# A graph-attention layer: block sums in chains, nodes ordered by one-hot products, first rows gathered ahead of the loop

## The chip, the cores and the metric

The kernel runs on one core of a Trainium2 chip. The metric is device time in microseconds (us) for one execution. Before the change it took 1119.08 us, the median of three runs (1115.03 to 1124.09). "Fast" is the state of a run in which nothing disturbed it; comparisons use fast runs.

## The reference, cut to what matters

Four graph layers work on 2708 nodes with 128 features and a dense 2708 x 2708 matrix, all in float32. The change lies in layer 1, an attention layer:

```python
XW    = X @ W
s_col = XW @ a[0, :f];  s_row = XW @ a[0, f:]
den   = exp(leaky_relu(s_row[:, None] + s_col[None, :], 0.01))
num   = A @ den
att   = where(num != 0, den / where(num != 0, num, 1.0), 0.0)
H     = A @ (att @ XW)
```

`den` has a simple form: where `s_row + s_col` is positive it is a product of two exponentials, elsewhere a product of two others. So if the nodes are sorted by `s_col`, then for a block of neighbouring columns each row uses one form for the whole block, except for the few rows whose change-over falls into the block. The kernels use this.

## The kernel before

Nodes are sorted and cut into blocks (`NB`, of `BJ` columns; 43 blocks of 64 before). For each block the sum over the rows that do not change inside it is taken by one dense product over the whole matrix (two weight columns per block: "the pass"). It goes to `carry`, two rows per block. The pass goes through the matrix in six chunks of up to 512 columns; a panel is four tiles of 128 rows of one chunk, loaded together. The rows that change inside a block, at most `KC` = 126 of them, are gathered from memory one by one. Together they are 128 rows, which one product per block (`num`) weighs. Two blocks make one step, and the columns are done in two halves `h`.

The rows stand in a pool of three buffers, which layer 0, the pass and the loop share in turn:

```python
stream = ctx.enter_context(tc.tile_pool(name="stream", bufs=3))
```

The loop stands in one side of a branch. The other side serves data in which some block has more than 126 such rows; it is not taken here.

```python
over = nc.values_load(flag[0:1, 0:1], min_val=0, max_val=N)
with tc.If(over > KC) as full:
    ...                                  # the dense way, not taken here
with full.Else():
    ...
    for h in range(2):
        hacc = ops.tile([P, 3 * CW], F32, tag="hacc", name="hacc")
        for q in range(NQ):
            rows = stream.tile([P, 2, HALF], F32, tag="strip", name="rows")
            for n, b in enumerate(pair):
                nc.gpsimd.indirect_dma_start(          # 126 rows of the matrix
                    out=rows[:KC, n, :], in_=adj_half[:, :],
                    in_offset=bass.IndirectOffsetOnAxis(ap=slot_i[h][:KC, b : b + 1], axis=0), ...)
                nc.sync.dma_start(rows[KC : KC + 2, n, :], carry[2 * b : 2 * b + 2, ...])
            for c0, w, bufs in ((0, WIDE, 2), (WIDE, NARROW, 1)):
                num = ops.tile([P, w], F32, tag=f"num{w}", name="num", bufs=bufs)
                ...                      # num[block] = lw[block].T @ rows
                mix(w, q, num, ...)      # 1/num, weights, hacc += xws.T @ err
```

## Time and profile before

| part of the profiled run before | from, us | length, us |
|---|---|---|
| layer 0 and the ordering by ranks | 0 | 438 |
| start and pass for block sums | 438.1 | 110.6 |
| loop, first `num` product to the copy after the last `hacc` | 548.7 | 232.5 |
| layers 2 and 3 with the rest of layer 1 | 781.2 | 338.2 |

These are two groups of the page (line, engine, operation, count, busy time in us and mean in ns, then the engine's idle time just before them and what ended most of it), and then TensorE's rows of one loop step (start, duration):

```profile
L1035 POOL DMA_INDIRECT rows<-in_adjT,slot_i x86 | 120.7, 1404 | 107.9 <-PE num L1048 79.9
L1048 PE MATMUL num<-rows,lw 128*64 128x512 f32 (+2 forms) x516 | 117.0, 558 | 6.7 <-DMA rows<-carry 3.7
```

```profile
638.13 2.50 PE L1048 MATMUL num<-rows,lw 128*64 128x330 f32 x12
640.56 2.54 PE L977 MATMUL hacc<-err,xws 128*128 128x512 f32 x6
```

GpSimd waits for TensorE to release a buffer, 79.9 us in all. The products are idle 6.7 us in total, 3.7 of them for the carried rows.

### The profile page before, as it was taken

How to read it: one execution, taken by the hardware profiler on the slowest of the kernel's cores; microseconds unless marked ns; L12 is line 12 of the kernel's file. 1: busy time of each engine (PE TensorE's matmuls, PEld its weight loads, DVE VectorE, ACT ScalarE, POOL GpSimd, SP SyncE). 2: the span in 40 equal slices, each digit the busy share in tenths (PEclk: the TensorE clock that was granted, in tenths of full speed). 3: DMA queues.
4: the chain of work that ended last, by engine and by line, in shares of the span. 5: the costliest groups of instructions: out<-in, count | busy, mean ns of one | idle time of the engine just before them, and what ended most of it. 6: DMA issues, size and time to landing. Idle time of an engine off the chain costs nothing.

```text
span 1119.4 us, 10743 instructions
## 1 busy us (share of the span) xinstructions
PE 1044.2 (93%) x3495; PEld 494.5 (44%) x3495; DVE 642.7 (57%) x1381; ACT 306.1 (27%) x569; POOL 299.4 (27%) x296
## 2 busy tenths in 40 slices
PE   0899999999999975999799999998999999999997
PEld 0346544444345654333333333333444644465445
DVE  6885549999636679403099999997311212122132
ACT  0000145555202434000165656664110100011000
POOL 4000000000477772772355655660010100000000
PEclk9999999999999995999999999998999999998999
DMA  9996320000576660797545534454475766563754
GB/s 349 354 316 222 125 101 1 1 0 1 178 274 201 184 207 13 230 304 236 164 121 148 176 96 129 164 171 142 150 236 186 227 227 219 173 227 117 263 166 129
DMA packets 110245, 193.89 MB, mean 173 GB/s; under 512 B 14156, under 2 KB 47106, under 8 KB 109926
## 3 DMA queue, kind: packets, MB, share of 16 engines
q1 hardware_dynamic: 91046, 151.12, 40.7%
q0 software_dynamic: 19136, 42.01, 12.0%
q8 instruction: 29, 0.48, 0.2%
q14 instruction: 34, 0.28, 0.1%
HBM read 217.20 MB, written 4.30 MB: 198 GB/s over the span
## 4 chain that ended last, share of the span: by engine, by line
PE 51%; issue 4%; DMA 4%; DVE 2%; POOL 1%; ACT 1%; POOLq 0%; DVEq 0%; ACTq 0%
PE acc L186 32%; PE hacc L977 8%; PE num L1048 8%; DMA rows<-in_adjT,slot_i 2%; DMA part<-in_adjT 1%; PE mis L259 1%; POOL rows L1035 1%; DVE mask L692 1%; PE mis L1110 0%; PE mis L1063 0%; DMA got<-y_rows,where 0%; ACT junk L710 0%; ACT hT L220 0%; PE mis L1076 0%; DVE mask L697 0%
## 5 line engine op out<-in xcount | busy, mean ns | idle before, releaser
L186 PE MATMUL acc<-part,y 128*128 128x512 f32 (+2 forms) x384 | 156.0, 550 | 2.1 <-DMA part<-in_adjT 1.6
L1035 POOL DMA_INDIRECT rows<-in_adjT,slot_i x86 | 120.7, 1404 | 107.9 <-PE num L1048 79.9
L1048 PE MATMUL num<-rows,lw 128*64 128x512 f32 (+2 forms) x516 | 117.0, 558 | 6.7 <-DMA rows<-carry 3.7
L977 PE MATMUL hacc<-err,xws 128*128 128x512 f32 (+3 forms) x264 | 113.6, 567 | 2.2 <-DVE err L972 1.8
L574 PE MATMUL acc<-zT,z 128*128 128x512 f32 (+4 forms) x264 | 106.9, 552 | 0.0
L602 POOL DMA_INDIRECT got<-y_rows,where x88 | 93.0, 1057 | 29.6 <-issue 11.9
L186 PEld LDWEIGHTS acc<-part,y 128*128 128x128 f32 x384 | 70.4, 191 | 64.5 <-issue 53.9
L970 DVE TENSOR_TENSOR err<-inv,num 128x1024 f32<-128x1024 f32 (+1 forms) x88 | 74.5, 856 | 27.1 <-DMA rows<-in_adjT,slot_i 21.0
L966 ACT ACTIVATE inv<-num 128x1024 f32<-128x1024 f32 (+1 forms) x88 | 64.3, 734 | 88.4 <-PE num L1048 86.6
L575 ACT COPY key<-acc 128x512 f32<-128x512 f32 (+3 forms) x132 | 70.2, 534 | 58.1 <-issue 29.8
L392 PE MATMUL acc<-part,y 128*128 128x512 f32 (+2 forms) x192 | 82.4, 582 | 2.2 <-DVE y L233 2.2
L977 PEld LDWEIGHTS hacc<-err,xws 128*128 128x128 f32 (+1 forms) x264 | 47.1, 192 | 80.4 <-issue 41.8
L186 PE MATMUL acc<-part,lc 128*86 128x512 f32 (+2 forms) x192 | 76.2, 553 | 3.3 <-DVE lc L876 2.5
L186 PE MATMUL acc<-part,xs 128*128 128x512 f32 (+2 forms) x192 | 78.6, 552 | 0.1
L972 DVE SCALAR_TENSOR_TENSOR err<-gb,g_inv,err 128x1024 f32<-128x1024 f32 (+1 forms) x88 | 77.1, 918 | 0.0
L536 POOL TENSOR_TENSOR y<-xs,d2inv 128x2176 f32<-128x2176 f32 (+1 forms) x2 | 4.6, 2322 | 264.3 <-ACT d2inv L534 264.3
L186 PE MATMUL acc<-part,mixed 128*128 128x512 f32 (+2 forms) x192 | 75.0, 545 | 0.2 <-DMA part<-in_adjT 0.2
L971 DVE SCALAR_TENSOR_TENSOR err<-err,inv 128x1024 f32<-128x1024 f32 (+1 forms) x88 | 71.8, 857 | 0.0
L574 PEld LDWEIGHTS acc<-zT,z 128*128 128x128 f32 (+1 forms) x264 | 47.0, 186 | 53.8 <-issue 48.4
L220 ACT COPY hT<-acc 128x512 f32<-128x512 f32 (+2 forms) x18 | 9.6, 534 | 220.1 <-PE acc L186 203.2
L967 ACT ACTIVATE inv<-inv 128x1024 f32<-128x1024 f32 (+1 forms) x88 | 67.3, 768 | 2.6
L576 DVE MAX8 near<-key 128x8 f32<-128x2708 f32 (+1 forms) x22 | 65.3, 2970 | 3.4 <-ACT key L575 3.4
(239 smaller groups left out, 1215.5 us busy)
## 6 DMA issues: line engine op xcount, KB each, us to landing
part<-in_adjT SPq DMA_DIRECT2D x102, 1024.0 KB
part<-in_adjT SPq DMA_DIRECT2D x24, 768.0 KB
part<-in_adjT SPq DMA_DIRECT2D x24, 552.0 KB
res<-in_adjT SPq DMA_DIRECT2D x4, 1280.0 KB
got<-y_rows,where POOLq DMA_INDIRECT x88, 3.9
rows<-in_adjT,slot_i POOLq DMA_INDIRECT x86, 5.8
rows<-carry SPq DMA_DIRECT2D x86, 10.6 KB
xws<-by_rank POOLq DMA_DIRECT2D x1, 1365.0 KB, 10.1
```

The costliest lines, as they stand in the source:

```text
L186: nc.tensor.matmul(accs[c][: lhsT.shape[-1], :w], lhsT=lhsT, rhs=src, start=start, stop=stop)
L392: nc.tensor.matmul(accs[c][:, : cw[c]], lhsT=y[:, i, :], rhs=src[:, : cw[c]], start=first, stop=last)
L574: nc.tensor.matmul(pks[c][:p, : cw[c]], lhsT=z2[:, :p], rhs=zT[:, cs], start=False, stop=True)
L575: nc.scalar.copy(key[:p, cs], pks[c][:p, : cw[c]])
L602: nc.gpsimd.indirect_dma_start(out=got[:p, :], out_offset=None, in_=y2_rows[:, :], in_offset=bass.IndirectOffsetOnAxis(ap=where[:p, t, k : ...
L967: nc.scalar.activation(inv[:p], inv[:p], AF.Exp, scale=-1.0)
L970: nc.vector.tensor_mul(err[:p], inv[:p], num[:p, :w])
L971: nc.vector.scalar_tensor_tensor(err[:p], err[:p], 2.0, inv[:p], op0=ALU.subtract, op1=ALU.mult)
L972: nc.vector.scalar_tensor_tensor(err[:p], gb[:p, col : col + w], g_inv[:p, q : q + 1], err[:p], op0=ALU.max, op1=ALU.mult)
L977: nc.tensor.matmul(haccs[:, o:e], lhsT=xws[:p, q, :D], rhs=err[:p, o:e], start=(q == 0), stop=(q == NQ - 1))
L1035: nc.gpsimd.indirect_dma_start(out=rows[:KC, n, :], out_offset=None, in_=adj_half[:, :], in_offset=bass.IndirectOffsetOnAxis(ap=slot_i[h][ ...
L1048: nc.tensor.matmul(num[n * BJ : n * BJ + bw[b], o:e], lhsT=lw[:, b, : bw[b]], rhs=rows[:, n, c0 + o : c0 + e], start=True, stop=True,)
```

## The change

The change has four aims. The pass becomes shorter: only the head of each chain of four blocks gets its sum from the dense product (22 columns of weights, padded to 32, in place of 86), and in the loop each block's product also yields the sum of the next block of its chain. Nodes are put in order by one-hot products on TensorE in place of 44 scatters by GpSimd through memory. The loop's order is written out by hand. And the rows of the first two steps are gathered ahead of the branch. The core of the diff, with cuts marked:

```diff
-BJ = 64
+BJ = 62
+CH = 4
 ...
-        by_panels(lambda i: lc[:, i, :, :].rearrange("p b s -> p (b s)"), end_carry)
+            nc.tensor.matmul(                                    # block sums, 4 column groups
+                sums_of[c][32 * g : 32 * g + 32, : cw[c]], lhsT=lc[rows, i, :], rhs=src, ...)
 ...                                                              # then one product folds the 4 groups
+        def into_places(out, at, values):                        # one-hot products for scatters
+                nc.vector.tensor_tensor(hot[:, :n, :], iota..., at[:, t0:t1, None]..., op=ALU.is_equal)
+                    nc.tensor.matmul(out[:, :width], lhsT=hot[...], rhs=values[...], ...)
-        scatter(by_slot, pos_u, val)
 ...
+    def load(i):
+        h, q = steps[i]
+        rows[i] = stream.tile([P, 2, HALF], F32, tag="strip", name="rows")
+        for n in range(2):
+            nc.gpsimd.indirect_dma_start(out=rows[i][:KC, n, :], ...)
+            nc.sync.dma_start(rows[i][KC : KC + 2, n, :], carry[2 * b : 2 * b + 2, ...])
+        if h == 0:
+            gather_xw(q)                                         # one more gather a step
+    load(0)
+    load(1)
     mT = wide.tile([P, N], F32, tag="wide", name="mT")
     over = nc.values_load(flag[0:1, 0:1], min_val=0, max_val=N)
     with tc.If(over > KC) as full:
 ...
     with full.Else():
-            for h in range(2): ... for q in range(NQ): rows = stream.tile(...)
+            with tc.manual_schedule(engines={e.engine for e in engines}):
+                find_num(0, "wide")
+                for i, (h, q) in enumerate(steps):
+                    if i + 2 < len(steps):
+                        load(i + 2)
+                    find_num(i, "narrow")
+                    find_num(i + 1, "wide")
+                    add(i - 1)
+                    ...
+                        keep(i, piece, errs[piece])              # a sum to the next block of the chain
```

## The prediction

> **What bounds the kernel now.** I read the busy shares first, then the table of stretches, the chain of waits, and last the timelines of single engines around layer 1.
>
> ```profile
> PE 1044.2 (93%) x3495; PEld 494.5 (44%) x3495; DVE 642.7 (57%) x1381; ACT 306.1 (27%) x569; POOL 299.4 (27%) x296
> ```
>
> TensorE is busy 93% of the time, so only removed TensorE work or a removed TensorE pause can count. The change lies wholly in layer 1, so I cut the span there: ordering, the pass for block sums, the start of the main loop, the loop, its last product, the rest.
>
> ```profile
> core 0: us, PE busy (x) PEld busy (x) DVE busy (x) ACT busy (x) POOL busy (x), PEclk, DMA share, GB/s
> 438.00:445.50 7.50, 0.70 (x5) 0.50 (x2) 6.51 (x23) 1.62 (x3) 5.61 (x7) 0.50 0.11 37
> 445.50:547.70 102.20, 101.32 (x270) 40.35 (x270) 27.33 (x95) 4.47 (x13) 55.16 (x54) 0.98 0.76 245
> 547.70:562.90 15.20, 9.44 (x30) 2.99 (x30) 4.50 (x6) 7.21 (x10) 5.44 (x6) 0.89 0.37 106
> 562.90:603.00 40.10, 38.82 (x132) 15.22 (x133) 38.66 (x49) 21.74 (x30) 20.53 (x15) 1.00 0.46 130
> 603.00:776.80 173.80, 171.99 (x613) 64.09 (x611) 169.07 (x210) 104.91 (x140) 90.20 (x62) 1.00 0.44 141
> 776.80:781.20 4.40, 4.37 (x6) 1.59 (x6) 0.43 (x1) 0.00 (x0) 0.00 (x0) 0.56 1.03 387
> 781.20:1119.40 338.20, 326.30 (x990) 169.31 (x990) 76.33 (x366) 30.49 (x88) 9.76 (x22) 0.97 0.59 193
> ```
>
> The block-sum pass takes 102.2 us with TensorE 99% busy: TensorE bounds it. The main loop runs from the first product at 548.7 to 781.2, 232.5 us for 44 steps; in its steady part TensorE is 99% and VectorE 97% busy. The first 15 us of the loop are bad, and the chain of waits says why:
>
> ```profile
> 538.73 3.01 DMA part<-in_adjT
> 546.09 11.52 DMA rows<-in_adjT,slot_i
> 588.89 10.59 DMA rows<-in_adjT,slot_i
> ```
>
> The first rows are gathered only when the pass gives its buffers back, and TensorE waits for them. Behind the pass (start, duration, engine, source line, then the idle time before) a second, hidden chain runs, of scatters and round trips through memory:
>
> ```profile
> 502.79 0.91 POOL L815 DMA_INDIRECT by_slot<-val,pos_u  x1 [0.30 <-issue]
> 513.12 0.55 POOL L808 DMA_DIRECT2D g_row<-g_c_d  x1 [3.34 <-DMA g_c_d<-g_c]
> 520.00 9.65 DVE L947 TENSOR_SCALAR lw<-g_row,slot_e,slot_f 128x64 f32<-128x64 f32 x43 [6.13 <-DMA g_row<-g_c_d]
> 541.91 1.11 POOL L1035 DMA_INDIRECT rows<-in_adjT,slot_i  x1 [11.42 <-DMA part<-in_adjT]
> ```
>
> The 44 scatters on GpSimd, some 1.28 us apart, last until 503.7; weights end at 529.65. So they cost nothing now, but a shorter pass alone would meet them. The change removes both.
>
> **What the Trainium skill says.**
> 1. "TensorEngine Tiling (Array Packing)", section Theoretical Speedup, gives up to 2x for an output of at most 64 and up to 4x for one of at most 32; "TensorE: Matmul & The Clock Gate", Part 3, has a measured 2.38x for three column tiles. The trace agrees for 64: a loop step has six num products, two blocks side by side, in 2.43 us, and three full-width products of the same length in 2.47 us. It has nothing for 32.
> 2. The same page, Part 1: an idle TensorE falls to half its clock. The trace agrees: 0.50 granted from 438 to 445.5, and the first block-sum products there start 0.85 us apart in the place of 0.43.
> 3. "GPSIMD Engine Reference", section 8, Key points: GpSimd shares its SBUF interfaces with VectorE and contends with VectorE instructions that have two SBUF inputs. The trace agrees: of two gathers per step the one that starts inside such an instruction takes 1.93 us, the other 1.06:
>
> ```profile
> 639.22 1.06 POOL L1035 DMA_INDIRECT rows<-in_adjT,slot_i  x1 [1.60 <-PE num L1048]
> 640.36 1.63 DVE L971 SCALAR_TENSOR_TENSOR err<-err,inv 128x1024 f32<-128x1024 f32 x2
> 640.59 1.93 POOL L1035 DMA_INDIRECT rows<-in_adjT,slot_i  x1 [0.30 <-issue]
> ```
>
> **The change part by part.** Times are on the clock of the profile before; ahead of 438 nothing changes.
>
> *Start of the pass.* Before, from the last rank product (438.1) to the first block-sum product took 7.4 us. Now only the 11 heads of chains are needed first: three operations on 242 elements (about 0.38 each, as 294 elements take 0.46), some 14 small ones of 0.1 to 0.15, three more of 0.38, and a wait for one product. I get 5.5 us: start at 443.6, gain 2.
>
> *Block sums.* The weights shrink from 86 columns to 32, and four tiles of rows go to four column groups. A 512-wide chunk was 22 products x 2 instructions x 0.427 = 18.8 us; at fourfold it is 4.7, and I take 5.7 with weight loads and switches. The pass falls to about 30 us of TensorE, so it is no longer bound by it. Its panels are 2048 x 2708 x 4 B = 22.2 MB; five (5.2 MB) are loaded ahead; the rest, 16.9 MB, needs 53 us at 320 GB/s, the best that this pass reaches in ten-microsecond stretches now (316, 320, 331).
>
> *Work put into the pass, in program order on TensorE.* That order decides: a wait for VectorE between chunks also stops the freeing of panels. I follow VectorE from 443.5: three operations on 968 elements at 1.17 (to 447), three on 484 at 0.65 (449), small ones (450), the blocks' numbers at 2.9 (453), in_b 1.3 and f_out (454.5). TensorE has done chunk 0, first cold, by about 452 and waits for in_b. Then 22 one-hot products put c and the nodes in order. A warm float32 product of 128 columns takes 0.22 us here (two instructions 0.11 apart in the last layer), so 5 us: to 461. Chunk 1 and its fold end at 468. Meanwhile VectorE makes the values (3.5) and the places: 20 dependent additions at 0.245, then three operations at 1.1, together 8.8; it is done at 473.5. The exponentials of c on all partitions need the same buffer as the places, so they fall to 476; the second 22 one-hot products (5.5) to 481; the exponentials of r to 484.5. Chunk 2 starts at about 485.
>
> From there only 8 to 12 of the 24 panels are in; with five buffers the transfers had stopped. Panels 13 to 23 are 8.55 MB, 26.7 us at 320 GB/s, so to 512; the last chunk, its fold and its copy add 3 to 4. The pass ends at about 516 in the place of 547.7: gain 31.5.
>
> *Start of the loop.* The slots are known from 482, so the first gathers leave when the last panels free the stream's buffers, near 507. An issue takes 1.36 with its gap, and a row transfer took 6.3 us in the median: rows at 515 to 517. First product about 518.
>
> *The loop.* Steps stay 44, TensorE work per step stays 4.90 us (2.43 + 2.47), VectorE's three operations stay 4.75. ScalarE gets one small multiply per step in the first half on top of 3.0. The chain in the loop has five to six steps from a sum to its use, some 25 us, against two small copies: hidden. Steady steps give 215.6; filling and draining the pipeline about 4; before, 43 steps from 563 to 776.8 took 4.97 each, so I keep 2 for stalls: 222. It ends at 740 in the place of 781.2.
>
> Sum: start of the pass and the pass 31.5, the loop with its start 232.5 + 1 - 224 = 9.5, together 41. With the unchanged 338.2: 740 + 338.2 = 1078. I say 1079.
>
> **The rivals.**
> 1. *The 32-column products don't overlap.* Then the pass keeps its 101 us and gets about 20 us of one-hot products and transposes on top: about 1130. For it: no 32-wide product in this trace. Against it: two 64-wide ones overlap fully. At 2.4-fold instead of 4 chunks 1 and 2 only lose about 3 us each: 1085.
> 2. *VectorE's order becomes the bound of the pass.* If its 22 us after chunk 0 grow to 30, or TensorE goes cold in the gaps and the one-hot products take 0.44, chunk 2 starts at 495 and all shifts by 10: 1089.
> 3. *GpSimd becomes the bound of the first half of the loop.* Three gathers per step are 3 x 1.36 = 4.1 us, plus about 0.9 of blocking twice: 4.9 to 5.6 against 4.90. At the bad end 22 x 0.7 = 15 us: 1094. For it: the 1.93 above. Against it: issues should fall into step with VectorE.
> 4. *The chain waits*: copies of sums plus reload stall each step. One microsecond in 44 steps would make 1123. Against it: the 25 us of room.
>
> **Range and chances.** Rivals 2 and 3 are likely in part and both point up; the downward side is a pass whose transfers never stop, ending near 503, or 1066. So 1079, range 1066 to 1098. The edge of "faster" is 1119.1 x 0.98 = 1096.7. Faster 0.87, within 2% 0.1, slower 0.03.
>
> **What would show it.** Right: the stretch from first block sum to first num product is about 75 us with TensorE well under 80% busy and transfers near 320 GB/s in its last 25 us; instructions of one 512 chunk start about 0.12 us apart; no wait over 5 us for rows at the start of the loop; TensorE's loop step 4.90. Wrong: TensorE busy throughout the pass (rival 1); chunk 2 later than 490 after a wait for VectorE (2); gathers over 1.6 us each with TensorE waiting for rows in the first 22 steps (3); TensorE waiting for carried rows (4).

## More of the kernel before

A single run of a kernel has the state "unknown", and such runs are marked.

A tile is taken from its pool by `.tile(...)`. The program builder then places it in one of the three buffers, and makes the first write wait until the last reader of the tile that was there is done. This is settled while the program is built, not on the chip.

## The result, and the profile after

The changed kernel is correct and takes **1503.24 us** (median of 4 runs, 1495.16 to 1505.74), beside 1117.55 for the kernel before on the same chip (4 runs). The ratio is 1.343, with a 95% interval of 1.335 to 1.351. Ratios here are the mean time of one kernel's fast runs over that of the other's fast runs of the same rounds, so not quite the ratio of the medians quoted.

The page of the changed kernel, its busy shares and the two groups that answer to those shown of before:

```profile
PE 1152.0 (77%) x3651; PEld 505.2 (34%) x3651; DVE 658.2 (44%) x1388; ACT 346.1 (23%) x632; POOL 259.9 (17%) x268
L1223 PE MATMUL num<-rows,lw 128*64 128x512 f32 (+1 forms) x528 | 256.7, 825 | 273.0 <-DMA rows<-in_adjT,slot_i 268.8
L1154 POOL DMA_INDIRECT rows<-in_adjT,slot_i x88 | 104.9, 1192 | 538.2 <-PE num L1223 474.9
```

The idle time ahead of the `num` products grew from 6.7 to 273.0 us, and what ended it is the gathered rows. At the same time GpSimd sat idle for 474.9 us until `num` products were done. Each waits for the other: that is a loop without room for anything in flight. The stretches place the loss (start:end, length, busy us of each engine, then granted TensorE clock, DMA share, GB/s):

```profile
444.80:524.60 79.80, 64.39 (x415) 30.02 (x415) 37.36 (x98) 21.84 (x54) 10.64 (x8) 0.86 0.65 221
524.60:537.00 12.40, 10.15 (x33) 3.48 (x33) 5.42 (x7) 7.41 (x9) 2.10 (x3) 0.88 0.33 104
537.00:1165.70 628.70, 359.75 (x760) 101.53 (x760) 213.45 (x258) 149.20 (x192) 122.09 (x101) 0.73 0.19 54
1165.70:1504.00 338.30, 326.61 (x992) 168.94 (x990) 76.55 (x366) 30.48 (x88) 9.76 (x22) 0.98 0.60 192
```

The pass and the rest are near the prediction. The loop, from the first `hacc` product to the start of the last, takes 628.7 us where before it took 217.4. A step is 628.7 / 43 = 14.6 us (43 intervals between 44 steps). One step in the timeline (start, duration, engine, line, in brackets the idle time before and what ended it):

```profile
711.21 0.78 PE L1223 MATMUL num<-rows,lw 128*64 128x330 f32 x4
712.29 1.06 POOL L1154 DMA_INDIRECT rows<-in_adjT,slot_i  x1 [9.47 <-PE num L1223]
713.65 1.06 POOL L1154 DMA_INDIRECT rows<-in_adjT,slot_i  x1 [0.30 <-issue]
717.56 1.97 PE L1223 MATMUL num<-rows,lw 128*64 128x512 f32 x2 [5.58 <-DMA rows<-in_adjT,slot_i]
719.99 2.96 PE L1223 MATMUL num<-rows,lw 128*64 128x512 f32 x6 [0.46 <-DMA rows<-in_adjT,slot_i]
722.88 2.54 PE L1132 MATMUL hacc<-inv,xws 128*128 128x512 f32 x6
725.35 0.78 PE L1223 MATMUL num<-rows,lw 128*64 128x330 f32 x4
```

The last `num` products of a step end at 711.99. Only then, 0.3 us later, does the gather for the next step leave; its rows land at 717.5; TensorE, idle for 5.58 us, starts at a lower clock (0.50 granted from 717.5 to 720.0, 1.00 from 722.9 on); at 725.35 the round begins again, 14.1 us later. So there is one buffer, not three. The two halves of the steps say that it is not the extra gather: only the first half has it, and from one `hacc` to the next a step takes 15.2 us there (303.7 us for 20 steps, from 552.43 to 856.16) and 14.7 in the second half (265.1 us for 18, from 872.19 to 1137.31).

The compiled program says where each tile lies. These are the start bytes of the `rows` tiles in their order:

```text
               step 0   step 1   step 2   step 3   step 4   step 5
before         122048   143744   132896   122048   143744   132896
changed        122048   143744   132896   132896   132896   132896
one load ahead 122048   143744   132896   143744   132896   143744
```

In the changed kernel the tiles of steps 0 and 1 are taken ahead of the branch and read inside it. From there on every tile inside the branch gets the one buffer that is left: 42 of the 44 lie at 132896. The last row is that of an experiment below with a single load ahead: two places in turn. Why the builder does not give the first places back inside the branch was not looked into; that it does not is what these addresses show.

The page "Perfetto Trace Analysis" of the Trainium skill, section Optimization Strategy, describes just this sign: the same gap repeating on an engine that should be saturated can mean that there is no room for the next tile. This trace agrees, with 6.3 us of it per step in the mean (268.8 / 43).

### The profile page after: what moved, and what is told of

Read it like the earlier page. It is cut to its first block, busy times and chain, and to the rows that moved or that the text cites. A ratio compares the mean times of both kernels' runs of the same rounds, so it can differ in the third digit from the quotient of the medians.

```text
span 1504.0 us, 11368 instructions
## 1 busy us (share of the span) xinstructions
PE 1152.0 (77%) x3651; PEld 505.2 (34%) x3651; DVE 658.2 (44%) x1388; ACT 346.1 (23%) x632; POOL 259.9 (17%) x268
## 5 line engine op out<-in xcount | busy, mean ns | idle before, releaser
L1223 PE MATMUL num<-rows,lw 128*64 128x512 f32 (+1 forms) x528 | 256.7, 825 | 273.0 <-DMA rows<-in_adjT,slot_i 268.8
L1117 DVE TENSOR_TENSOR err<-inv,num 128x1024 f32<-128x1024 f32 x88 | 75.5, 860 | 450.6 <-ACT inv L1110 450.5
L1223 PEld LDWEIGHTS num<-rows,lw 128*64 128x64 f32 x528 | 54.2, 182 | 439.0 <-DMA rows<-in_adjT,slot_i 362.2
L1154 POOL DMA_INDIRECT rows<-in_adjT,slot_i x88 | 104.9, 1192 | 538.2 <-PE num L1223 474.9
L1109 ACT ACTIVATE inv<-num,plain 128x1024 f32<-128x1024 f32 x88 | 80.5, 914 | 473.8 <-PE num L1223 473.7
L1132 PE MATMUL hacc<-inv,xws 128*128 128x512 f32 (+1 forms) x264 | 119.7, 591 | 2.0 <-DVE inv L1124 2.0
L1132 PEld LDWEIGHTS hacc<-inv,xws 128*128 128x128 f32 x264 | 50.8, 208 | 101.4 <-issue 97.7
L1124 DVE SCALAR_TENSOR_TENSOR inv<-gb,g_inv,inv 128x1024 f32<-128x1024 f32 x88 | 76.9, 914 | 0.0
L1121 DVE SCALAR_TENSOR_TENSOR inv<-err,inv 128x1024 f32<-128x1024 f32 x88 | 73.7, 877 | 0.0
L1110 ACT ACTIVATE inv<-inv 128x1024 f32<-128x1024 f32 x88 | 67.5, 768 | 2.8
L582 DVE FIND_INDEX8 where<-near,key 128x8 uint32<-128x2708 f32 (+1 forms) x22 | 65.4, 2972 | 0.0
```

Of the source, the lines that this page charges most:

```text
L1109: nc.scalar.activation(inv, num[:, :w], AF.Ln, scale=plain[:, 0:1], bias=plain[:, 1:2])
L1117: nc.vector.tensor_mul(err, inv, num[:, :w])
L1121: nc.vector.scalar_tensor_tensor(inv, err, 2.0, inv, op0=ALU.subtract, op1=ALU.mult)
L1124: nc.vector.scalar_tensor_tensor(inv, gb[:, col : col + w], g_inv[:, q : q + 1], inv, op0=ALU.max, op1=ALU.mult)
L1132: nc.tensor.matmul(haccs[:, o:e], lhsT=xws[:, q, :], rhs=inv[:, o:e], start=(q == 0), stop=(q == NQ - 1))
L1154: nc.gpsimd.indirect_dma_start(out=rows[i][:KC, n, :], out_offset=None, in_=adj_half[:, :], in_offset=bass.IndirectOffsetOnAxis(ap=slot_i[ ...
```

## The experiments

My theory after the result: **tiles taken ahead of the branch and used inside it keep their buffers for as long as the branch is being written, so the loop has one buffer left.** The rivals: the written-out order or the chain serializes the loop; the third gather per step makes GpSimd the bound; early gathers as such do harm.

The runs fell on two sorts of chip. On the first the kernel before takes 1160.06 us (8 runs); on the second 1117 to 1120. In the profiles of the slower chip the 40 us more lie ahead of the last rank product, so ahead of the change. Ratios to the kernel before on the same chip are comparable.

| run | chip's before, us | median, us (runs) | ratio (95%) |
|---|---|---|---|
| loads inside the branch | 1160.06 | 1140.66 (4) | 0.984 (0.981 to 0.987) |
| one load ahead, one inside | 1160.06 | 1219.96 (1, unknown) | |
| kernel before, two loads ahead | 1160.06 | 1527.1 (1, unknown) | |
| loads inside, third gather ahead of the branch | 1160.06 | 1159.28 (4) | 0.998 (0.994 to 1.002) |
| kernel before again | 1120.31 | 1119.01 (1, unknown) | |
| loads inside, chain's copies removed | 1120.31 | 1095.38 (4) | 0.980 (0.975 to 0.985) |
| loads inside, ordering one chunk later | 1120.31 | 1096.31 (4) | 0.979 (0.976 to 0.983) |
| several of these | 1120.31 | 1104.25 (4) | 0.987 (0.982 to 0.991) |
| no branch, early loads kept | 1120.17 | 1262.04 (4) | 1.127 (1.123 to 1.131) |
| loads inside the branch, again | 1120.17 | 1101.41 (6) | 0.986 (0.982 to 0.989) |
| ordering one chunk later, again | 1120.17 | 1096.91 (6) | 0.981 (0.977 to 0.985) |
| the same, weights earlier | 1120.17 | 1098.65 (6) | 0.981 (0.978 to 0.985) |
| no branch, one activation table | 1117.33 | 1101.61 (6) | 0.987 (0.983 to 0.991) |
| the same, ordering later, weights earlier | 1117.33 | 1098.10 (6) | 0.983 (0.979 to 0.986) |

### The loads moved into the branch

```diff
-    load(0)
-    load(1)
     mT = wide.tile(...)
     ...
             with tc.manual_schedule(engines={e.engine for e in engines}):
+                load(0)
+                load(1)
                 find_num(0, "wide")
```

> The changed kernel with the first two row loads moved from ahead of the branch to the first lines of the branch that runs. Theory A (rows held across the branch leave one stream buffer for all later loads, so each gather waits for the products of the step before it and TensorE waits for the gather): all three buffers rotate again, the loop step falls from 14.6 us to 4.9 to 5.1, and the time to 1083 to 1100 us. Theory B (the chain of passed-on sums, whose copy and reload stand between steps, sets the 14 us): the step stays near 14 and the time near 1500. Theory C (three gathers per step overload GpSimd): first half of the loop stays slow, second half fast, about 1300.

Measured: 1140.66 us on the slower chip, ratio 0.984; the whole loss is gone by moving two lines. A step is 226.5 / 43 = 5.3 us, a little above the 4.9 to 5.1 expected. Repeated later on the faster chip, to be compared with other runs there:

> The kernel with both loads inside the branch once more, for comparison on one chip: ratio 0.984 as the first time (0.980 to 0.988).

Measured: 1101.41 us, ratio 0.986. The compiled program gives the `rows` tiles the three places in rotation again. The loop of the second run, in the same stretch as above, and the waits for gathered rows (us and times; this view adds up all engines' waits, in the changed kernel 631.0 us in 162):

```profile
535.90:760.20 224.30, 216.68 (x760) 82.41 (x760) 208.19 (x258) 148.76 (x190) 139.36 (x97) 0.99 0.47 144
```

```profile
  DMA rows<-in_adjT,slot_i: 6.1, 10
```

This also splits the loss. Between the two loops lie 628.7 - 224.3 = 404 us, for the same 760 TensorE instructions. Idle time grew from 7.6 to 269.0, so by 261 us; the other 143 us are the same products running longer. The granted clock was 0.73 in the place of 0.99, which by itself would make some 294 us of 216.7 (216.7 x 0.99 / 0.73, an estimate from the two mean clocks). The step shown above holds a part of the rest: its second block's rows land only at 719.99, so the first products of the two blocks no longer run side by side. The gaps thus cost more than their own length.

### One load ahead, one inside

```diff
+    load(0)
     mT = wide.tile(...)
     ...
-                load(0)
                 load(1)
```

(against the version with both inside)

> The changed kernel with one row load ahead of the branch and the second inside: two buffers are left. Theory A: a gather waits for the products two steps before the step that uses it and has one step's work to hide behind; step 7 to 9 us, time 1190 to 1270 us, clearly between the changed kernel and e1_loads_in_branch. Theory B and C: as slow as the changed kernel.

Measured: 1219.96 us (one run). The loop's stretch takes 301.6 us, or 7.0 a step, between 5.3 with no load ahead (226.5 / 43, same chip) and 14.6 with two. With two buffers a gather has one step's time to land, and the wait for it remains in part:

```profile
  DMA rows<-in_adjT,slot_i: 128.3, 106
```

So the loss follows the number of buffers left, as a cause should.

### The kernel before with its first two loads ahead of the branch

```diff
+    first_rows = [load(0, 0), load(0, 1)]     # ahead of tc.If
     ...
-                    rows = stream.tile([P, 2, HALF], F32, tag="strip", name="rows")
-                    ...
+                    pair, rows = first_rows.pop(0) if first_rows else load(h, q)
```

> The kernel before with one part of the change alone: its first two row loads issued ahead of the branch. Theory A: rows again have one buffer in the branch; a step becomes a gather (about 6.5 us to landing) plus the products that give the buffer back, 9 to 13 us in the place of 4.97, and the time 1290 to 1480 us, though there are no chains and no third gather. Theories B and C: nothing of theirs is in it, so about 1110 us or a little less.

Measured: 1527.1 us (one run). This has no chain, no one-hot products, no written-out order and no third gather, and yet its loop takes 581.0 us for 43 intervals, 13.5 a step, even more than the 9 to 13 expected. Built again, its `rows` tiles lie as in the changed kernel, 42 of 44 in one place. The gaps look the same in its timeline:

```profile
810.24 1.97 PE L1053 MATMUL num<-rows,lw 128*64 128x512 f32 x2 [6.29 <-DMA rows<-in_adjT,slot_i]
823.28 1.97 PE L1053 MATMUL num<-rows,lw 128*64 128x512 f32 x2 [5.37 <-DMA rows<-in_adjT,slot_i]
```

So the two early loads are sufficient for the loss, and moving them is sufficient to cure it. As a control of the chip, the kernel before was also submitted as a run of its own, unchanged:

> The kernel before, unchanged, for its profile on the chip of this set of runs. All theories: the time of the kernel before in the same rounds; from the last rank product to the first num product 110 us, the loop 232 us, the rest 338 us, as in the first profile, and whatever is slower here than there lies ahead of layer 1.

Measured: 1119.01 us (one run), among the 1114.35 to 1122.57 of its other runs there.

### No branch at all

"Early" and "across a branch" are still one thing so far. This run keeps the early loads of the changed kernel and takes the branch away: the `Else` side is written straight on, and the `If` side is dropped (no block has more than 126 rows in this data).

```diff
     load(0)
     load(1)
     mT = wide.tile(...)
-    over = nc.values_load(flag[0:1, 0:1], min_val=0, max_val=N)
-    with tc.If(over > KC) as full:
-        ...
-    with full.Else():
-        with (...):
+    with (...):
             ...                               # the loop, unchanged
```

> The changed kernel with its loads 0 and 1 where they were, but with the branch for overfull blocks taken away, so that the loop stands in the same straight program as the loads. My theory (two tiles taken ahead of the branch and used inside it are not given back while the branch lasts): the three buffers rotate again, a loop step is near 5.2 us, rows are waited for only at the start, the ratio to the kernel before is 0.97 to 0.99. Rival (early loads as such do the harm, through the order of GpSimd's or SyncE's queue or through rows read before the sums are in place): a step stays near 14 us, the ratio near 1.34. If early gathers are worth something by themselves, the first num product comes up to 5 us earlier after the pass than in the kernel with its loads inside the branch, run beside this one.

Measured: 1262.04 us, ratio 1.127. Neither theory had said this. The profile shows why: the waits for rows are gone, but a new cost came. The preload of an activation table ahead of the loop did not hold its place in the straight program, and every change between logarithm and exponential loads a table (groups of the page, then the waits for rows):

```profile
L1109 ACT ACT_TABLE_LOAD x88 | 112.9, 1283 | 10.9 <-PE num L1184 9.3
L1110 ACT ACT_TABLE_LOAD x88 | 112.9, 1283 | 1.5
```

```profile
  DMA rows<-in_adjT,slot_i: 3.5, 2
```

ScalarE was busy for 367.8 of the 380.3 us of this loop, so it set the step of 8.8 us. The `rows` tiles rotate over the three places in the compiled program. But at 8.8 us a step, a row transfer of 6.1 us in the median would be hidden by less than three buffers, so the run did not answer its question. The edit had changed two things. The next run takes the second one back, by pinning the preload in its place:

```diff
-        nc.scalar.preload_act_table_set("natural_log_exp_and_others")
+        tc.keep_in_program_order(nc.scalar.preload_act_table_set("natural_log_exp_and_others"))
```

> The kernel without the branch and with its early loads where the change put them, as before, but with ScalarE's preload of one table for logarithm and exponential fixed in its place ahead of the loop, so that the 176 table loads of 1.28 us (225.8 us on ScalarE, which set the 8.9 us step of the run without it) are gone. My theory (the branch holds the two early tiles): steps of 5.0 to 5.3 us, rows waited for only at the start of the loop, ratio 0.975 to 0.985, time about 1095 on a chip where the kernel before takes 1119. Rival (early loads cost by themselves, hidden behind the table loads in the run before): steps of 6 us or more and waits for rows throughout, 1140 or more.

Measured: 1101.61 us, ratio 0.987 (just above the 0.975 to 0.985 expected), beside 0.986 for the loads inside the branch (intervals overlap). The loop's stretch:

```profile
536.10:762.60 226.50, 218.62 (x760) 83.06 (x760) 210.47 (x259) 148.71 (x191) 109.53 (x98) 0.99 0.50 147
```

A step is 226.5 / 43 = 5.27 us. The theory stands: early loads do no harm by themselves; early loads **across a branch** do. And they do no good either. The first gather of rows left 72.3 us after the first block sum without the branch (516.70), and 70.6 us after it with the loads inside (516.03): standing earlier in the program did not let it leave earlier. With the loads inside, moreover, the first product's wait is put down to the carried rows and not to the gathered ones:

```profile
524.41 6.26 PE L1221 MATMUL num<-rows,lw 128*64 128x512 f32 x20 [4.04 <-DMA rows<-carry]
```

There an earlier gather alone would gain nothing. Without the branch the carried rows were issued from 514.38, ahead of the pass's last fold at 518.39, and the first product's wait, 3.30 us, is put down to the gathered rows. What holds the first loads back was not tested; without the branch SyncE waits 4.7 us for block-sum products before it issues the first carried rows, which fits buffers that the pass still holds. The first product came 78.0 us after the first block sum without the branch, and 79.0 with it.

### What else did not come: the chain

The loop without the loss is 222 us in the prediction and 236.3 in the profile of the repeated run (524.4 to 760.7). To find the chain's part, its copies from one block to the next are left out, and the pass's sums go to all four blocks of a chain. The sums are then wrong, and the amount of other work is the same. (The comparison with the reference passed all the same. So that comparison does not vouch for the chain's sums.)

```diff
-                    if b % CH:
+                    if False and b % CH:
     ...
-            nc.vector.tensor_copy(sel...[:, :, :2], fold...)
+            for m in range(CH):
+                nc.vector.tensor_copy(sel...[:, :, 2 * m : 2 * m + 2], fold...)
```

(against the version with both loads inside)

> e1_loads_in_branch without the copies that pass the sums on (every block is given its chain head's sums; a wrong result on purpose, the same work on all other engines). If the passing on of sums costs the loop something, through the copies or the wait for the reload, the loop is shorter than in e1_loads_in_branch (239.5 us) by 5 to 12 us and the ratio to the kernel before falls from 0.984 to about 0.975; if it is hidden, the ratio stays within 0.003 of 0.984.

Measured: 1095.38 us, ratio 0.980, beside 0.984 and 0.986 for the same kernel with its chain. The loop's stretch is 216.4 us:

```profile
538.40:754.80 216.40, 214.04 (x760) 80.52 (x760) 208.31 (x259) 148.60 (x190) 139.39 (x98) 1.00 0.47 145
```

From the first `num` to the start of the last `hacc` it is 231.3 us without the chain's copies and 235.8 with them, and 231.7 in the kernel before. But the same loop with its copies took from 231.1 to 239.1 us in the profiles of the versions with loads inside the branch (231.1 in the one with the weights earlier), the ratio of 0.980 lies between the two that were expected, and the intervals overlap. So a cost of the chain of some 4.5 us is possible and not shown.

### What else did not come: the third gather

All 22 gathers of feature rows are made ahead of the branch, none in the loop.

```diff
-        if h == 0:
-            gather_xw(q)                     # in load(i)
+    for q in range(NQ):
+        gather_xw(q)                         # ahead of the branch
```

(against the version with both loads inside)

> As e1_loads_in_branch, and all 22 gathers of the ordered XW rows go ahead of the branch, so that a loop step has two gathers in both halves. If three gathers per step cost the first half of the loop something (rival 3 of the prediction), this is up to 15 us faster than e1_loads_in_branch; if GpSimd keeps step anyway, the two are within 3 us, and the early gathers may even delay the first rows a little.

Measured: 1159.28 us, ratio 0.998, a miss as an improvement. The loop's stretch is 222.9 in the place of 226.5 us, and the same loop with its third gather took from 218.7 to 226.5 in other profiles; a cost of the third gather is not seen there. But the first product comes 16 us later after the first block sum (94.0 us in the place of 77.8). It is not GpSimd's queue that held the first rows: the gathers of feature rows were issued by 543.3, and GpSimd then sat idle for 28.45 us until the first row gather at 571.75. The pass itself was longer: its last fold started 86.6 us after the first block sum in the place of 73.0. Why the early gathers lengthen the pass was not tested.

### The order of the pass

The second set of one-hot products and the exponentials stop TensorE between chunks 1 and 2, while panels wait to be released. Here they come one chunk later.

```diff
-            if c == 1:
+            if c == 2:                       # g_row, listed(), gb
     ...
-            if c == 2:
+            if c == 3:                       # weights()
```

(against the version with both loads inside)

> e1_loads_in_branch with the listing of the nodes and the exponentials one chunk later (after chunk 2 in the place of chunk 1), the weights after chunk 3. If TensorE's program order in the pass is what stops the panels (in e1_loads_in_branch TensorE spends 16 us between chunks 1 and 2 on ordering, with all buffers full), the transfers go on and the pass ends 8 to 13 us earlier: ratio about 0.975. If the transfers bound the pass anyway, the ratio stays at 0.984.

Measured: 1096.31 us, ratio 0.979, between the two that were expected. The pass up to the first `num` took 78.3 us in the profile of this run and 74.8 in that of the repeated one below, beside 77.8 and 79.0 with the order unchanged: less than the 8 to 13 us hoped for, and near the scatter of the profiles. In the repeated run's profile TensorE waits ahead of the last-but-one fold, because 22 weight operations of 7.36 us in all stand ahead of a copy on ScalarE. The next edit moves them ahead of it, and three kernels ran together on one chip:

```diff
             if c == 2:
                 ...
+                weights(lw, g_row)
-            if c == 3:
-                weights(lw, g_row)
```

> The ordering work one chunk later, once more, for comparison on one chip: 0.979 as the first time, so some 5 us below the kernel with both loads inside the branch.

> As the one before, but the 22 weight operations of ScalarE stand right behind the exponentials, one chunk earlier, so that they no longer lie ahead of the copy of chunk 4's sums. There TensorE was idle for 4.3 us; if that pause set the end of the pass, the first num product comes some 4 us earlier and the ratio is 0.975. If the panels' transfers set the end of the pass, nothing changes: 0.979.

Measured: 1096.91 us (0.981) and 1098.65 us (0.981). That fold's wait fell as wanted, first the version without, then the one with the edit:

```profile
509.16 1.46 PE L1083 MATMUL mis<-tot,sel 128*88 128x384 f32 x2 [4.30 <-ACT tot L1081]
```

```profile
508.80 0.88 PE L1083 MATMUL mis<-tot,sel 128*88 128x384 f32 x2 [0.62 <-ACT tot L1081]
```

but the fold itself starts only 1.1 us earlier after the first block sum (62.8 in the place of 63.9), and the pass up to the first `num` is 72.9 in the place of 74.8 us. The medians do not differ by more than their scatter. So most of the hoped-for 4 us did not come.

Two attempts to add things up missed. One took the order above, four early feature gathers and another split of panels over the two pools:

```diff
-load_panel(g, 0, more_pool if g % 5 > 2 else stream)
+load_panel(g, 0, more_pool if g % 5 in (2, 3) else stream)
 ...
+    for q in range(4):
+        gather_xw(q)                         # ahead of the branch, the others in the loop
```

> e7_order_after_chunk_2, and the gathers of XW rows kept out of the way of the first row loads: four ahead of the branch, the others four steps ahead in the loop; the stream's buffers are the first of the last five panels to come free. The first rows come 2 to 4 us earlier and steps 2 and 3 of the loop don't wait for theirs (some 6 us in e1_loads_in_branch): ratio about 0.968, the fastest of all.

Measured: 1104.25 us, ratio 0.987. Its first row gathers left at 508.5, yet its first `num` product came only at 530.2, after 8.7 us in which TensorE waited for nothing that the profile names; ScalarE's first instruction of the branch, a table load, came as late (529.39, after 7.43 us of the same). I did not find out what held them. The other takes the order, the weights and no branch:

```diff
-            if c == 1:
+            if c == 2:                       # g_row, listed(), gb, and now weights()
-            if c == 2:
-                weights(lw, g_row)
```

(against the version without the branch and with one table)

> The same, with the ordering work one chunk later and the weights right behind the exponentials. If what sets the start of the loop is the panels' transfers, then a gather that leaves as soon as the buffers are free brings the first num product forward by up to 4 us against the kernel with the branch: ratio 0.97 to 0.98. If nothing is gained by it, 0.981.

Measured: 1098.10 us, ratio 0.983: nothing gained over the version with the branch. The best correct version is the change with its two loads inside the branch and the ordering one chunk later, at 0.979 and 0.981 in two sets: about 2% faster than the kernel before (intervals 0.976 to 0.983 and 0.977 to 0.985), and at 0.73 of the time of the change as it was made (0.981 / 1.343). Against the version with only the loads moved (0.984 and 0.986) its gain is some 5 us in both sets, with overlapping intervals.

## Why the prediction was wrong

It said 1079 us, with a range of 1066 to 1098, and it was 1503. Its points in order:

**The step that failed** is that of the loop: "Steps stay 44, TensorE work per step stays 4.90 us", with its sum "222. It ends at 740". The TensorE instructions stayed as counted, but the step was 14.6 us, as the loop had one buffer for rows in the place of three. Nothing in the prediction looks at where the `rows` tiles lie once the first two are taken ahead of the branch. It treated the early loads as a pure shift in time ("the first gathers leave when the last panels free the stream's buffers"). None of its four rivals is about buffers, though its view of the kernel before showed that GpSimd waits for buffers in each step, so that their number is what keeps transfers ahead. The runs with 0, 1 and 2 loads ahead (5.3, 7.0 and 14.6 us a step), the kernel before with two loads (13.5) and the version without a branch (5.27) show it. The loop took 641.6 us from its first product to the copy after its last, 420 more than predicted; all other terms together err by some six.

**The start of the pass**: predicted 443.6, measured 444.8. Right within 1.2 us.

**The block sums**: right. Four 32-wide column groups overlap; 32 instructions of 512 columns took 3.64 us, 0.114 each, where 0.12 was predicted. Rival 1 fell. In all the block sums took 37.8 us of TensorE in the place of about 30, for the most part because the first two chunks ran below the full clock (next point): the same 32 instructions of chunk 1 took 6.32 us.

```profile
489.14 3.64 PE L1056 MATMUL acc<-part,lc 128*32 128x512 f32 x32
520.02 0.70 PE L1083 MATMUL mis<-tot,sel 128*88 128x276 f32 x2 [0.53 <-ACT tot L1081]
524.58 4.56 PE L1223 MATMUL num<-rows,lw 128*64 128x512 f32 x12 [3.86 <-issue]
```

**The work put into the pass**: right in kind, a little short. Chunk 2 started at 489.1 (predicted 485), the pass ended at 520.7 (516), the first `num` came at 524.6 (518). TensorE was granted 0.66 to 0.78 of its clock from 444.8 to 472, as rival 2 had it in part; the one-hot products that were to take 5 us took 7.4. The test "transfers near 320 GB/s" in the last part held: 325 GB/s from 489.1 to 509.1. The test that TensorE be "well under 80% busy" did not: it was 64.39 of 79.8 us, 81%.

**Gain of the loop, 9.5 us**: this would not have come without the failed step either. With the buffers given back the loop is 231.5 to 239.5 us in the profiles of the versions with loads inside the branch, about as long as before (232.5). On top of 44 steps at 4.90 us, 215.6 in all, the prediction allowed 6 for filling, draining and stalls; the loop of the repeated run took 20.7 more than 215.6. Its start is one part: from the first `num` to the first `hacc` 11.5 us pass at a granted clock of 0.85. The rest was not divided up, and what the chain costs stays open.

**Early gathers**: credited with a start of the loop without waits, with the first gather leaving near 507. It left at 518.13, and the gain could not be measured. The prediction read the waits at the start of the loop as waits for gathered rows; the page of the kernel before puts 3.7 of the 6.7 us ahead of `num` down to the carried rows.

**Two sums in the prediction are off.** In rival 3, 4.1 us and 0.9 of blocking once or twice make 5.0 to 5.9, not 4.9 to 5.6, so its bad end is some 1100, above the stated range. And 20 additions at 0.245 with three operations at 1.1 make 8.2, not 8.8. Neither bears on the step that failed.

**The rest**, 338.2: measured 337.8. With the failed step undone the change takes 1101 us: the pass shortened by 24 us (103.2 to 79.0, first block sum to first `num`), and nothing more. That is 22 above the prediction and still just outside of its range.

## What to carry to other kernels

Before trusting that a loop keeps its pace, look in the compiled program at where its rotating tiles lie, above all when a change takes some of them ahead of a branch or another scope and uses them inside. In a profile the sign is a pair of waits that name each other: the loader idle until the consumer is done, and the consumer idle until the load lands, once per step. And an edit that removes one suspect (here the branch) can bring a cost of its own: look at the profile of an experiment before reading its time.

## What the Trainium skill lacked or had wrong

- No page says that a tile taken ahead of a branch and read inside it keeps its buffer while the branch is being written. Here it cost 14.6 in the place of 5.2 us a step. "Perfetto Trace Analysis", section Optimization Strategy, has the sign (consistent bubbles) but not this cause.
- "TensorEngine Tiling (Array Packing)", section Theoretical Speedup, has up to 4x for outputs of at most 32, without a measurement; this case shows 0.114 us against 0.427 for an instruction of 512 columns, 3.7 times. "TensorE: Matmul & The Clock Gate", Part 3, has 2.38 times for three column tiles only.
- "ScalarE: Activation LUTs", section What ACT_TABLE_LOAD costs, gives 1.28 us for the load and 1.38 more for a drain at each switch. The load is 1.283 us here; the drain does not show in the version without the branch, in which ScalarE goes from one operation through the load to the next with gaps of 0.02 us (710.38 + 1.28, next 711.68), and sat idle 12.5 us in all in the 380.3 us of the loop.
